# Expert rows written into their experts' regions block by block, with their result's row beside them, instead of an index built after the last block

## The chip, the cores and the metric

The kernel runs on one core of one Trainium2 chip. A core has TensorE (PE), whose weight loads are listed apart as PEld, VectorE (DVE), ScalarE (ACT), GpSimd (POOL) and SyncE (SP). Each runs its own instructions in order and waits for the others by semaphores. The metric is device time in microseconds; the figure before is the median of nine runs. The page beside it is of one profiled execution, and its span reaches from the first to the last instruction.

## What is computed

Float32 throughout: `x` has 4 sequences of 1024 tokens with 128 features, 4096 tokens in all. A modulated layer norm feeds a layer whose small network is trained by gradient steps along the sequence (a scan of 1024 steps, the same for all four sequences), then a second modulated layer norm feeds a mixture of experts: 8 experts with 512 hidden features, the best 2 of each token, and one shared expert for all.

```
h = layernorm(x) * (1 + ca) + sa
k, v = split(h @ W_KV)                       # per token
params = scan(gradient step on mean((mlp(params, k_t) - v_t)**2))
x = x + ga * mlp(params, h @ W_Q)            # mlp = silu(h W1 + b1) W2 + b2

h = layernorm(x) * (1 + cb) + sb
probs = softmax(h @ w_router.T)              # 8 experts
vals, idx = top_k(probs, 2)
gates = one_hot(idx) * vals summed           # 0 for experts not chosen
acc = gelu(h @ Ws1.T + bs1) @ Ws2.T + bs2    # the shared expert
y_e = gelu(h @ W1[e].T + b1[e]) @ W2[e].T + b2[e]
acc = acc + sum over e of gates[e] * y_e
x = x + gb * SCALE * acc
```

## The kernel before

P is 128. The 4096 tokens are 32 columns of 128 tokens, or 8 blocks (`NBLK`) of 512 tokens. The stages, which follow one another:

1. *Front.* Loads, first layer norm, keys and values. Constants are made on POOL in numbered steps (L180 on).
2. *Scan.* 162 iterations of up to 7 steps each, a chain through PE, ACT and DVE. SP issues the loads of Gram products (`gm`, L334) that later iterations need, and groups of keys; the order is written out by hand.
3. *First layer's output, second norm, logits.* A pipeline over the blocks: `mlp_a` (L846) and `mlp_b` (L852) apply the trained network, `residual` (L861) turns the result and adds it to `x_sb`, `ln_stats` (L230) makes mean and `rstd`, with the statistics from DVE and the rest, a power among it, on POOL, `ln_scaled` (L252) and `ln_turned` (L262) make `hT`. `rows` (L870) multiplies each column of `hT` by the identity beside the router weights: one matmul turns the tokens back into rows and gives their logits. The rows go to `h_tab` in DRAM in token order, the logits to `pl`.
4. *Routing.* When all logits are there: softmax, the best two experts by two maxima (`hit`, L955 to L963), running counts of tokens by expert over all columns (`cum`), the place of each (token, choice) pair in an order sorted by expert in which every expert starts a new tile of 128 rows. There are at most `NTL` = 71 tiles. The order is turned round, from place to token, by 128 matmuls `inv` (L1062) of one-hot matrices that DVE builds (`sel` L1048, `val` L1053). `rows_i` is for each place the row of the result table, twice the token plus the choice, and `toks_i` is half of it. Between them PE does the 32 `shared_up` steps (L922), the shared expert's first layer.
5. *Expert loop.* 71 tiles; for tile t: gather its 128 rows from `h_tab` by `toks_i` (L1081, POOL, four tiles ahead), load the expert's two weight matrices (L1090 and L1092, SP, three ahead, the expert read into a register from `whose_i`), turn the rows (`pt` L1099, `xT` L1101), first layer (`ph` L1108, `hs` L1112), second layer (`py` L1120, `yg` L1124), scatter the results to `y_tab` by `rows_i` (L1125, POOL). Four `shared_down` steps (L934; matmuls `ps` L938 and L940, additions L945 and L946), the shared expert's second layer, stand before the loop, and 28 in it, one in every second tile.
6. *Tail.* `y_tab` is loaded back, each token's two results are weighed with its gates and added, and the output is stored.

Stages 3 to 6 stand in `manual_schedule()`: instructions go to the engines in the order of the code. Pools give memory out again when they are closed; an instruction that writes reused memory waits for the former readers. The PSUM pools have three (`pa`), two (`epy`), two (`ept`) and one (`epl`) buffers.

In the loop, before:

```
for t in range(NTL):
    if t + AHEAD < NTL:
        gather(t + AHEAD)
    if t + 3 < NTL:
        ws[t + 3] = weights(t + 3)
    nxt = turn_in(t + 1) if t + 1 < NTL else None
    hs = up(t, xT, ws[t][0])
    if t % 2 and downs:
        shared_down(downs.pop(0))
    if prev:
        down(*prev)
```

Of the kernel before, what the change touches and what calls it, by code (L numbers as in the profile page):

```python
# [10 lines left out]
F32 = mybir.dt.float32  # L11
# [6 lines left out]
P = 128  # L18
# [7 lines left out]
def kernel(  # L26
# [35 lines left out]

    NTL = TOP_K * NTOK // P + NE - 1
    WIN = 32
# [98 lines left out]
    cum = [const.tile([P, NT // 2 + NT, NE], F32, name=f"cum{i}") for i in range(2)]  # L163
# [16 lines left out]
    def constants(n):  # L180
# [27 lines left out]
        elif n == 4:  # L208
            sort_c["lane"] = iota("lane", [P], [[1, P]])
            sort_c["part"] = iota("part", [1], [[0, 1]], mult=1)  # L210
            sort_c["row1"] = iota(
                "row1", [TOP_K, NT], [[1, TOP_K], [TOP_K * P, NT]], base=1, mult=TOP_K
            )
            sort_c["edge"] = iota("edge", [NT], [[P, NT]])
            nc.gpsimd.memset(tri, 1.0)
            nc.gpsimd.affine_select(
                out=tri, in_=tri, compare_op=ALU.is_gt, fill=0.0, base=0, pattern=[[1, P]],
                channel_multiplier=-1,
            )
            for i in range(2):  # L220
                nc.gpsimd.memset(cum[i][:, 0:NT // 2, :], 0.0)
                nc.gpsimd.memset(ends[i][:, 0:NE // 2], 0.0)

# [47 lines left out]
    hT = hpool.tile([P, NBLK, BT], F32, name="hT")  # L271

    with tc.tile_pool(name="scanbig", bufs=1) as sbig, tc.tile_pool(
# [66 lines left out]
        for i, eng in enumerate((nc.gpsimd, nc.vector)):  # L340
            eng.memset(k_rows[i], 0.0)

# [140 lines left out]
        lane, part, row1, edge = (sort_c[n] for n in ("lane", "part", "row1", "edge"))  # L483
# [9 lines left out]
        with tc.tile_pool(name="s_ps", bufs=1, space=PSUM) as sps, tc.manual_schedule():  # L493
# [71 lines left out]
            for i in range(NI):  # L565
# [34 lines left out]
                if i + PF < NI and i:  # L600
                    gms[i + PF] = load_products(i + PF, nc.sync)
                more = todo.pop(0) if todo else None
# [106 lines left out]


# [92 lines left out]
    ffd = ctx.enter_context(tc.tile_pool(name="ffd", bufs=1, space=DRAM))  # L803

    h_tab = ffd.tile([NTOK, D], F32, name="h_tab")
    y_tab = ffd.tile([TOP_K * NTOK, D], F32, name="y_tab")
    with ExitStack() as stage, tc.tile_pool(
# [10 lines left out]


        xg_bufs = [small(f"xg{i}", [D]) for i in range(6)]  # L820
        hit = [small(f"hit{k}", [NT, NE]) for k in range(TOP_K)]
# [4 lines left out]
        gpad = small("gpad", [NT, P // BLK])  # L826
        b2g = small("b2g", [B])
# [3 lines left out]
        nc.gpsimd.memset(gpad, 0.0)  # L831
        nc.gpsimd.memset(gpad[:, :, NE:NX], 1.0)
        for xg in xg_bufs:
            nc.gpsimd.memset(xg, 0.0)


# [5 lines left out]
        ep = stage.enter_context(tc.tile_pool(name="q_sb", bufs=2))  # L842
        pl = small("pl", [NT, NE])
        aq, yq, xh = {}, {}, {}

        def mlp_a(j):  # L846
            pz = bank(pa, "pz", "a", [BT])
            nc.tensor.matmul(pz, lhsT=wqa, rhs=hT[:, j, :], start=True, stop=True)  # L848
            aq[j] = ep.tile([P, BT], F32, name="aq")
# [11 lines left out]
        def residual(j):  # L861
            pyt = bank(ept, "pyt", "t", [BLK, D])
            y = yq.pop(j)
            for i in range(BLK):
                nc.tensor.transpose(pyt[:, i, :], y[:, ts(i, P)], ident)  # L865
            xs = x_sb[:, ts(j, BLK), :]
            nc.vector.tensor_tensor(xs, pyt, xs, ALU.add)
            ln_stats(ep, j)

        def rows(j):  # L870

            hr = ep.tile([P, BLK, D], F32, name="hr")
            for i in range(0, BLK, 2):
# [6 lines left out]
                nc.scalar.copy(hr[:, i:i + 2, :], ptr[:, :, 0:P])  # L880
                c = j * BLK + i
                nc.scalar.copy(pl[:, c:c + 2, :], ptr[:, :, P:P + NE])
            nc.sync.dma_start(
                h_tab[j * BT:(j + 1) * BT, :].rearrange("(c p) d -> p c d", p=P), hr
            )

        for s in range(NBLK + 5):
            if 0 <= s - 2 < NBLK:
                residual(s - 2)
            if 0 <= s - 3 < NBLK:  # L890
                xh[s - 3] = ln_scaled(ep, s - 3)
            if 0 <= s - 4 < NBLK:
                j = s - 4
                ln_turned(bank(ept, "pt", "t", [BT]), xh.pop(j), j, 3, 4, hT[:, j, :])
            if s < NBLK:
                mlp_a(s)
            if 0 <= s - 1 < NBLK:
                mlp_b(s - 1)
            if 0 <= s - 5:
                rows(s - 5)  # L900

        stage.close()
        ep = stage.enter_context(tc.tile_pool(name="e_sb", bufs=2))


        def wide(v_):
            return v_.unsqueeze(2).to_broadcast([P, NT, NE])

        def full(name):
            return small(name, [NT, NE])  # L910

        mx, sm, pr, left, taken = (
            small("mx", [NT]), small("sm", [NT]), full("prob"), full("left"), full("taken")
        )
        nc.vector.tensor_reduce(mx, pl, AX.X, ALU.max)
        nc.vector.tensor_tensor(pr, pl, wide(mx), ALU.subtract)
        nc.scalar.activation(pr, pr, AF.Exp)

# [14 lines left out]

        def shared_down(c):  # L934
# [13 lines left out]
        shared_up(10)  # L948
        nc.vector.tensor_reduce(sm, pr, AX.X, ALU.add)
        nc.vector.reciprocal(sm, sm)  # L950
        nc.vector.tensor_tensor(pr, pr, wide(sm), ALU.mult)
        rest = pr
        for k in range(TOP_K):
            top = gate[:, k, :]
            nc.vector.tensor_reduce(top, rest, AX.X, ALU.max)  # L955
            nc.vector.tensor_tensor(hit[k], rest, wide(top), ALU.is_equal)
            nc.vector.tensor_tensor(hit[k], hit[k], desc.to_broadcast([P, NT, NE]), ALU.mult)
            nc.vector.tensor_reduce(mx, hit[k], AX.X, ALU.max)
            nc.vector.tensor_tensor(hit[k], hit[k], wide(mx), ALU.is_equal)
            if k + 1 < TOP_K:  # L960

                rest = left
                nc.vector.scalar_tensor_tensor(left, hit[k], -4.0, pr, ALU.mult, ALU.add)  # L963

        nc.vector.tensor_tensor(taken, hit[0], hit[1], ALU.add)

        def from_(t, d):
            return t[:, NT // 2 - d:NT // 2 - d + NT, :]

        nc.vector.tensor_copy(from_(cum[0], 0), taken)  # L970
        at, d = 0, 1
        while d < NT:
            nc.vector.tensor_tensor(
                from_(cum[1 - at], 0), from_(cum[at], 0), from_(cum[at], d), ALU.add
            )
            at, d = 1 - at, 2 * d
        inc = from_(cum[at], 0)
        pp = bank(epl, "pp", "l", [2, NE])
        for i, m in enumerate((tri, ones)):
            nc.tensor.matmul(pp[:, i, :], lhsT=m, rhs=inc[:, NT - 1, :], start=True, stop=True)  # L980
        shared_up(10)
        excl = from_(cum[1 - at], 0)
        nc.vector.tensor_tensor(excl, inc, taken, ALU.subtract)
        cnt = small("cnt", [2, NE])
        nc.vector.tensor_copy(cnt, pp)

        over = small("over", [NE, NT])
        nc.vector.tensor_tensor(
            over, cnt[:, 1, :].unsqueeze(2).to_broadcast([P, NE, NT]),
            edge.unsqueeze(1).to_broadcast([P, NE, NT]), ALU.is_gt,  # L990
        )
        tiles = small("tiles", [NE])
        nc.vector.tensor_reduce(tiles, over, AX.X, ALU.add)
        h0 = NE // 2
# [257 lines left out]
```

## Time and profile before

| what | value |
|---|---|
| median of nine runs (lowest to highest) | 924.31 us (923.91 to 932.17) |
| the profiled execution's own time | 924.51 us |
| its span | 922.3 us |
| mean granted TensorE clock | 0.965 |
| PE, DVE, ACT, POOL busy | 88%, 53%, 53%, 63% |
| scan (stage 2) | 60 to 568.6 us of the span |
| stage 3 | 568.6 to 609.3 |
| routing | 609.3 to 654.8 (the first gather) |
| expert loop, first to last `ph` | 664.9 to 884.3 |
| mean of one gather (L1081), one scatter (L1125) | 1025 ns, 1018 ns |

In a view of windows a row is one stretch of time, and for each engine the busy time and number of instructions in it. In a timeline a row is one instruction, or several of one line run together: start, duration, engine, line, what it writes and reads, and in brackets how long the engine had been idle and what ended that. Rows marked SPq or POOLq are an engine's issuing of DMAs. PE's matmuls overlap, so that the start of one to the start of the next tells what one costs.

### The profile page before, as it was taken

The numbers are of one execution on the slowest core, as the hardware profiler recorded it, in microseconds if no ns is written. First come the engines' busy times: TensorE is split into PE (matmuls) and PEld (weight loads), VectorE is DVE, ScalarE is ACT, GpSimd is POOL, SyncE is SP. The second block draws the span as 40 slices with busy tenths as digits, with TensorE's granted clock in tenths as the row PEclk, the third lists the DMA queues.
The fourth block names the chain that finished last, engine by engine and source line by source line (L and its number), as shares of the span: only waits on it lengthen the run. The fifth ranks groups of instructions, "written<-read, shape, count | busy, mean of one in ns | idle before, by whom it ended". The sixth has DMA issues, their size and how long they took to land. (4 is left out here: it accounts for less than half of the span.)

```text
span 922.3 us, 21051 instructions
## 1 busy us (share of the span) xinstructions
PE 808.5 (88%) x6132; PEld 736.4 (80%) x6132; DVE 487.6 (53%) x1843; ACT 491.9 (53%) x1595; POOL 582.6 (63%) x1593
## 2 busy tenths in 40 slices
PE   4689999999999999999999997889888888887740
PEld 3456899999999999999999994546787878887740
DVE  5434566666666666666666663679422221212127
ACT  2554566666666666666666663675233333332333
POOL 6831587778777877787778784520266666666630
PEclk9989999999999999999999998999999999989775
DMA  5363200110001001100011000022056656656655
GB/s 137 104 172 116 82 24 23 24 43 25 23 24 42 25 22 24 42 25 22 24 24 25 21 7 1 27 67 92 29 188 209 202 196 214 216 177 205 197 172 171
DMA packets 77859, 79.84 MB, mean 87 GB/s; under 512 B 9904, under 2 KB 56990, under 8 KB 77744
## 3 DMA queue, kind: packets, MB, share of 16 engines
q1 hardware_dynamic: 68880, 65.58, 23.5%
q0 software_dynamic: 5600, 10.02, 3.7%
q10 hardware_dynamic: 3264, 2.89, 1.0%
q8 instruction: 50, 0.82, 0.4%
q14 instruction: 65, 0.53, 0.2%
HBM read 61.83 MB, written 17.53 MB: 86 GB/s over the span
## 5 line engine op out<-in xcount | busy, mean ns | idle before, releaser
L1112 ACT ACTIVATE hs<-ph,b1t 128x128 f32<-128x128 f32 x284 | 80.8, 370 | 147.8 <-PE pt L1099 80.9
L692 POOL COPY dl<-dz 24x128 f32<-24x128 f32 (+2 forms) x158 | 44.5, 281 | 124.0 <-DVE dz L669 124.0
L1081 POOL DMA_INDIRECT xg<-h_tab,toks_i x71 | 72.8, 1025 | 70.5 <-DVE toks_i L1077 49.1
L1125 POOL DMA_INDIRECT y_tab<-yg,rows_i x71 | 72.3, 1018 | 68.3 <-DVE xT L1101 54.5
L530 DVE SCALAR_TENSOR_TENSOR u<-pu,u 128x130 f32<-128x130 f32 x158 | 46.5, 294 | 112.8 <-PE pu L517 112.8
L1120 PE MATMUL py<-w2t,hs 128*128 128x128 f32 x568 | 80.3, 286 | 18.0 <-issue 12.3
L1108 PE MATMUL ph<-xT,w1t 128*128 128x128 f32 x568 | 80.0, 286 | 13.3 <-DVE xT L1101 13.2
L1120 PEld LDWEIGHTS py<-w2t,hs 128*128 128x128 f32 x568 | 72.0, 198 | 21.8 <-issue 15.4
L1108 PEld LDWEIGHTS ph<-xT,w1t 128*128 128x128 f32 x568 | 71.5, 197 | 19.0 <-DVE xT L1101 19.0
L555 POOL TENSOR_TENSOR sums<-sums,sq 128x48 f32<-128x48 f32 (+2 forms) x315 | 86.3, 293 | 0.0
L633 ACT COPY ad<-z 128x128 f32<-128x128 f32 (+3 forms) x162 | 43.0, 265 | 66.4 <-PE z L631 66.4
L596 PE MATMUL y<-nm,er 128*128 128x128 f32 (+3 forms) x322 | 73.4, 309 | 3.4 <-DVE nm L584 2.7
L498 PE MATMUL z<-kT,a 128*128 128x156 f32 (+3 forms) x324 | 72.9, 307 | 0.0
L539 ACT COPY c<-pv 128x128 f32<-128x128 f32 x158 | 42.0, 266 | 52.7 <-PE pv L535 49.8
L627 PE MATMUL y<-ae,c 128*128 128x128 f32 (+3 forms) x324 | 69.1, 295 | 0.0
L945 DVE TENSOR_TENSOR sh<-ps,gb_rep 128x128 f32<-128x128 f32 x32 | 9.3, 292 | 112.1 <-PE ph L1108 64.5
L508 ACT ACTIVATE vb<-vT,v 128x128 f32<-128x128 f32 (+3 forms) x162 | 65.0, 401 | 1.2 <-DVE dr L656 0.9
L548 POOL TENSOR_TENSOR sq<-ch 128x104 f32<-128x104 f32 (+1 forms) x158 | 56.9, 360 | 12.4
L612 ACT ACTIVATE ae<-z,u 128x156 f32<-128x156 f32 (+3 forms) x162 | 62.8, 388 | 1.9 <-POOL el L693 0.9
L579 PE MATMUL z<-gm,dz 128*128 128x128 f32 (+3 forms) x322 | 62.9, 277 | 0.2
L662 PE MATMUL da<-v,ae 128*128 128x128 f32 (+3 forms) x324 | 62.9, 276 | 0.0
L547 POOL TENSOR_TENSOR ch<-ae 128x104 f32<-128x104 f32 (+1 forms) x158 | 62.4, 395 | 0.0
(294 smaller groups left out, 2433.4 us busy)
## 6 DMA issues: line engine op xcount, KB each, us to landing
w1t<-in_e_w1t_dram SPq DMA_DIRECT2D x71, 256.0 KB
w2t<-in_e_w2t_dram SPq DMA_DIRECT2D x71, 256.0 KB
gm<-g_dram SPq DMA_DIRECT2D x151, 64.0 KB
g_dram<-gw SPq DMA_DIRECT2D x29, 206.0 KB
x_sb<-in_x_dram SPq DMA_DIRECT2D x8, 256.0 KB
k_dram<-kr SPq DMA_DIRECT2D x8, 256.0 KB
h_tab<-hr SPq DMA_DIRECT2D x8, 256.0 KB
hs_all<-y_tab ACTq DMA_DIRECT2D x4, 512.0 KB
```

The costliest lines, as they stand in the source:

```text
L498: nc.tensor.matmul(z[:, 0:n], lhsT=wa, rhs=kc[:, o * B:o * B + n], start=True, stop=alone)
L508: nc.scalar.activation(vb[:, 0:n], vc[:, o * B:o * B + n], AF.Identity, bias=v[:, D:D + 1], scale=-1.0,)
L555: nc.gpsimd.tensor_tensor(t, t, x_[:, :, c0:c1], ALU.add)
L579: nc.tensor.matmul(z[:, 0:rn], lhsT=dz_p[0:ro, :], rhs=gms.pop(i)[0:ro, 0:rn], start=False, stop=True,)
L596: nc.tensor.matmul(y[:, 0:rn], lhsT=er_p[0:ro, :], rhs=nm[0:ro, 0:rn], start=True, stop=False,)
L627: nc.tensor.matmul(y[:, 0:rn], lhsT=wc, rhs=at[:, 0:rn], start=not prev, stop=True)
L662: nc.tensor.matmul(da[0:rn, :], lhsT=et[:, 0:rn], rhs=v[:, 0:D], start=not prev, stop=True)
L1081: nc.gpsimd.indirect_dma_start(out=xg_bufs[t % 6][:], out_offset=None, in_=h_tab[:, :], in_offset=bass.IndirectOffsetOnAxis(ap=toks_i[:, t ...
L1108: nc.tensor.matmul(ph[:, f, :], lhsT=w1t[:, ts(f, P)], rhs=xT, start=True, stop=True)
L1112: nc.scalar.activation(hs[:, f, :], ph[:, f, :], AF.Gelu_apprx_tanh, bias=b1t[:, t, f:f + 1])
L1120: nc.tensor.matmul(py, lhsT=hs[:, f, :], rhs=w2t[:, f, :], start=(f == 0), stop=(f == NFC - 1))
L1125: w = nc.gpsimd.indirect_dma_start(out=y_tab[:, :], out_offset=bass.IndirectOffsetOnAxis(ap=rows_i[:, t:t + 1], axis=0), in_=yg[:], in_off ...
```

## The change

*Regions.* `h_tab` is replaced by `h_sort`, a DRAM table with a region of 4096 rows for each expert and 128 rows more. A row has 144 values: the 128 features and 16 times the number of the row of the result table (`HW = D + 16`). A `blank` tile, whose rows hold zeros and a row number outside the result table, is written over all of `h_sort` in 33 transfers (`fill`); 16 more (`together`) copy each expert's first and second layer side by side into `e_all` in DRAM. These 49 transfers are issued by SP in the scan, one in every third iteration from the ninth on.

*Routing by blocks.* Stages 3 and 4 become one loop over the blocks. After the logits of a block, `choose` finds the best two experts from the logits themselves, `rank` gets each pair's place from the counts of this block and those carried from the blocks before (matmuls with `tri` and `ones`), `send` scatters the rows of the block from SBUF to their places, eight indirect DMAs of 128 rows by POOL, and `count` carries the counts on. The statistics of the second norm are all on DVE (`stats`, the inverse root by a bit trick and three Newton steps), its scaling on ACT (`turned_rows`). `rows` copies each row twice, once for each choice, into one of five buffers `hrs`, whose last 16 columns hold the result's row. All 32 `shared_up` steps stand in this loop. Softmax, gates and the tables of tiles come after it; the place-to-token matmuls and their one-hot matrices are gone.

*The loop.* A tile's rows are 128 rows of `h_sort` in order: SP loads them from a place read into a register, as it loads both layers' weights with one DMA from `e_all`. `to`, the row numbers for the result's scatter, is copied from the rows themselves. Weights and rows are fetched four tiles ahead. 16 `shared_down` steps stand before the loop and 16 in it, spread evenly.

```diff
@@ constants
+            nc.gpsimd.memset(blank, 0.0)
+            nc.gpsimd.memset(blank[:, :, D:HW], float(4 * TOP_K * NTOK))
@@ before the scan
+        def fill(n):
+            r0, r1 = n * P * FILL, min((n + 1) * P * FILL, NE * NTOK + P)
+            nr = (r1 - r0) // P
+            nc.sync.dma_start(
+                h_sort[r0:r1, :].rearrange("(p r) d -> p r d", r=nr), blank[:, 0:nr, :]
+            )
+        def together(n):
+            e, k = n // 2, n % 2
+            nc.sync.dma_start(
+                e_all[:, e, k * NFC * P:(k + 1) * NFC * P],
+                e_w2t[:, e, :, :].rearrange("p c d -> p (c d)") if k else e_w1t[:, e, :],
+            )
@@ in the scan
+                if early_work and i >= 9 and i % 3 == 0:
+                    do, n = early_work.pop(0)
+                    do(n)
@@ the pool of stages 3 and 4
+        qp = ExitStack()
+        ep = qp.enter_context(tc.tile_pool(name="q_sb", bufs=2))
+        HR = 5
+        hrs = [ep.tile([P, BLK, TOP_K, HW], F32, name=f"hr{i}", bufs=1) for i in range(HR)]
@@ stats, in place of ln_stats
+            for i in range(BLK):
+                nc.vector.bn_stats(st[:, i, :], x_sb[:, j * BLK + i, :])
+            for i in range(BLK):
+                nc.vector.bn_aggr(ag[:, i, :], st[:, i, :])
...
+            for _ in range(3):
+                nc.vector.tensor_tensor(t, r[at], r[at], ALU.mult)
+                nc.vector.scalar_tensor_tensor(t, t, -0.5, var, ALU.mult, ALU.mult)
+                nc.vector.scalar_tensor_tensor(r[1 - at], t, 1.5, r[at], ALU.add, ALU.mult)
+                at = 1 - at
@@ rows
-                nc.scalar.copy(hr[:, i:i + 2, :], ptr[:, :, 0:P])
-            nc.sync.dma_start(
-                h_tab[j * BT:(j + 1) * BT, :].rearrange("(c p) d -> p c d", p=P), hr
-            )
+                nc.scalar.copy(
+                    hrs[j % HR][:, i:i + 2, :, 0:D],
+                    ptrs[i // 2][:, :, 0:P].unsqueeze(2).to_broadcast([P, 2, TOP_K, D]),
+                )
@@ choose, for each of the two choices
+                nc.vector.tensor_reduce(top, rest, AX.X, ALU.max)
+                nc.vector.tensor_tensor(hit, rest, over_e(top), ALU.is_equal)
+                nc.vector.tensor_tensor(hit, hit, desc.to_broadcast([P, BLK, NE]), ALU.mult)
+                nc.vector.tensor_reduce(first, hit, AX.X, ALU.max)
+                nc.vector.tensor_tensor(hit, hit, over_e(first), ALU.is_equal)
@@ rank
+            nc.tensor.matmul(rk, lhsT=tri, rhs=taken[j], start=True, stop=False)
+            for d in range(1, BLK):
+                nc.tensor.matmul(
+                    rk[:, d:BLK, :], lhsT=ones, rhs=taken[j][:, 0:BLK - d, :],
+                    start=False, stop=False,
+                )
+            nc.tensor.matmul(rk, lhsT=ones, rhs=carry[j], start=False, stop=True)
@@ send
+            for i in range(BLK):
+                for k in range(TOP_K):
+                    w = nc.gpsimd.indirect_dma_start(
+                        out=h_sort[:, :], out_offset=bass.IndirectOffsetOnAxis(
+                            ap=place_i[:, k, i:i + 1], axis=0
+                        ),
+                        in_=hrs[j % HR][:, i, k, :], in_offset=None,
+                        bounds_check=NE * NTOK - 1, oob_is_err=False,
+                    )
@@ the order of stages 3 and 4
+        for j in range(NBLK):
+            choose(j)
+            rank(j)
+            if j + 1 < NBLK:
+                turned_rows(j + 1)
+            if j + 3 < NBLK:
+                mlp_b(j + 3)
+            if j >= 1:
+                shared_up(2)
+            if j + 1 < NBLK:
+                rows(j + 1)
+            if j + 2 < NBLK:
+                added(j + 2)
+            send(j)
+            count(j)
+            if j + 2 < NBLK:
+                stats(j + 2)
+            if j + 3 < NBLK:
+                residual(j + 3)
+            if j >= 1:
+                shared_up(3)
@@ after softmax, gates and the tables of tiles
+        qp.close()
+        ep = stage.enter_context(tc.tile_pool(name="e_sb", bufs=2))
@@ the loop's loads
-            nc.gpsimd.indirect_dma_start(
-                out=xg_bufs[t % 6][:], out_offset=None, in_=h_tab[:, :],
-                in_offset=bass.IndirectOffsetOnAxis(ap=toks_i[:, t:t + 1], axis=0),
-                bounds_check=NTOK - 1, oob_is_err=False,
-            )
+        def weights(e):
+            wt = ep.tile([P, 2, NFC, P], F32, name="wt", bufs=5)
+            nc.sync.dma_start(
+                wt.rearrange("p k f d -> p (k f d)"),
+                e_all[:, bass.ds(e, 1), :].rearrange("p e f -> p (e f)"),
+            )
+            return wt
+        def tokens(at):
+            xg = ep.tile([P, HW], F32, name="xg", bufs=6)
+            nc.sync.dma_start(xg, h_sort[bass.ds(at, P), :])
+            return xg
@@ turn_in
+            to = ep.tile([P, 1], I32, name="to", bufs=6)
+            nc.vector.tensor_copy(to, xg[:, D:D + 1])
@@ the loop
+        LATE = 16
+        vals = [values(t) for t in range(AHEAD)]
+        ws = {t: weights(vals[t][0]) for t in range(AHEAD)}
+        xs = {t: tokens(vals[t][1]) for t in range(AHEAD)}
+        for c in range(NT - LATE):
+            shared_down(c)
+        downs = list(range(NT - LATE, NT))
+        cur = turn_in(xs.pop(0))
+        for t in range(NTL):
+            if t + AHEAD < NTL:
+                e, at = values(t + AHEAD)
+                ws[t + AHEAD] = weights(e)
+                xs[t + AHEAD] = tokens(at)
+            nxt = turn_in(xs.pop(t + 1)) if t + 1 < NTL else None
+            hs = up(t, cur[0], ws[t])
+            if downs and (t + 1) * LATE // NTL > LATE - len(downs):
+                shared_down(downs.pop(0))
+            if prev:
+                down(*prev)
```

## The prediction

> **What bounds the kernel now.** I read the page's slices first (TensorE, PE below, is busy nine tenths of almost every slice), then the busy time by stage, then the timeline inside the stages that the change touches. The windows below begin at the end of the scan; columns are engine busy time with instruction counts, granted clock, DMA share and GB/s.
>
> ```profile
> core 0: us, PE busy (x) PEld busy (x) DVE busy (x) ACT busy (x) POOL busy (x), PEclk, DMA share, GB/s
> 568.60:609.30 40.70, 34.90 (x163) 21.86 (x164) 21.17 (x73) 23.38 (x55) 20.39 (x64) 0.92 0.14 40
> 609.30:655.00 45.70, 42.00 (x195) 26.14 (x195) 39.34 (x77) 23.86 (x36) 0.18 (x1) 1.00 0.18 58
> 655.00:665.00 10.00, 7.74 (x56) 6.26 (x55) 3.06 (x11) 2.34 (x4) 6.04 (x6) 1.00 0.14 39
> 720.00:760.00 40.00, 33.16 (x269) 30.49 (x267) 9.10 (x38) 13.75 (x49) 24.79 (x25) 1.00 0.62 200
> ```
>
> The first two rows are what the change fuses: 86.4 us in which PE is busy 76.9 and POOL nearly idles in the second half. The fourth is the expert loop: the clock is full, DMA works 62% of the time, and PE still shows seven microseconds of idling in forty. Its matmul records overlap in their modelled ends, so the true slack is read from starts:
>
> ```profile
> 722.52 0.30 PEld L938 LDWEIGHTS ps<-eb,gT 128*128 128x128 f32 x2
> 722.85 1.06 PE L940 MATMUL ps<-sw,hs_all 128*128 128x128 f32 x8
> ...
> 723.63 0.97 PEld L1120 LDWEIGHTS py<-w2t,hs 128*128 128x128 f32 x8
> ...
> 724.52 0.14 PEld L1099 LDWEIGHTS pt<-iw,xg 128*128 128x128 f32 x1
> 724.63 0.27 PE L1099 MATMUL pt<-iw,xg 128*128 128x128 f32 x1
> 724.64 0.97 PEld L1108 LDWEIGHTS ph<-xT,w1t 128*128 128x128 f32 x8
> ...
> 725.64 1.02 POOL L1081 DMA_INDIRECT xg<-h_tab,toks_i  x1 [0.31 <-issue]
> 725.98 0.29 DVE L945 TENSOR_TENSOR sh<-ps,gb_rep 128x128 f32<-128x128 f32 x1 [4.01 <-PE ph L1108]
> ...
> 727.72 1.14 ACT L1112 ACTIVATE hs<-ph,b1t 128x128 f32<-128x128 f32 x4 [3.69 <-PE pt L1099]
> ```
>
> From start to start a shared down costs PE 723.63 − 722.52 = 1.11 us, four `py` pairs 724.52 − 723.63 = 0.89, a `pt` 0.12, four `ph` pairs 0.89 again: a tile is 1.90. The first `ph` starts at 664.9 and the last at 884.3: 219.4 us for 70 steps and 28 downs, of which PE needs 70 × 1.90 + 28 × 1.11 = 164.1. So 55.3 us, 0.79 a step, is waiting. The last lines show on what: `ps` is over at 723.9 but DVE reads it at 725.98, `ph` of 724.74 is over by 725.8 but ACT starts at 727.72. PE's completions reach the other engines about 2 us late. In the stage before the loop, with as busy a PE, `ph` of the shared expert ends at 652.02 and ACT starts at 652.05. What differs is POOL's indirect DMAs, two a tile in the loop, back to back:
>
> ```profile
> 658.95 1.00 POOL L1081 DMA_INDIRECT xg<-h_tab,toks_i  x1 [0.30 <-issue]
> 660.26 1.00 POOL L1081 DMA_INDIRECT xg<-h_tab,toks_i  x1 [0.30 <-issue]
> 661.56 1.00 POOL L1081 DMA_INDIRECT xg<-h_tab,toks_i  x1 [0.30 <-issue]
> ```
>
> During this row of gathers, with no other traffic to speak of, a `ps` already waited 1.8 us for DVE (ended 661.7, read 663.49). That the indirect DMAs cause the lateness is inference; that it goes with them is what the trace shows.
>
> **The change, part by part.** *Front and scan.* 49 more transfers go through SP's queue in the scan, one every third iteration: 33 of 590 KB that blank `h_sort` and 16 of 256 KB, DRAM to DRAM, that put both layers of an expert side by side. The scan is a chain PE, ACT, DVE of 2.96 us an iteration, with DMA mostly idle (slices 6 to 23: tenths of 0 to 2). Iterations that load 337 KB of keys took 2.897 or 2.985 us beside 2.897 without: 0 to 0.09 each. For 49 transfers that is 0 to 4.4 us; on SP one issue of 0.3 to 0.45 us precedes loads that are fetched iterations ahead. Two memsets of 128x1152 on POOL in the front are, by the 0.95 us of a 128x1024 one, 0 to 2 us. I take 2.2 for all of it, both ends kept.
>
> *The fused stage.* Per block of 512 tokens DVE gets choose (12 operations of about 0.21 at 128x32), the residual add 0.69, statistics (8 of 0.28 and less, 13 of 0.21, in place of POOL's chain with its 1.04 us power), send and count (5 of 0.21): 8.5 us. ACT gets 8.2 (four scaled rows 1.2, `hT` 0.78, four copies 1.6, `aq` and `yq` 1.5, four shared activations of 0.69, blank ids), PE 8.4. The 128 `inv` matmuls (15.4 us of PE), the 21.7 us of `sel` and `val` on DVE, and the stores of `h_tab` go. POOL gets eight scatters a block, each 128 rows of 576 B. A gather or scatter of 128 rows has a period of 1.30 to 1.33 us here, so 64 cost 64 × 1.32 = 84.5 us: 10.6 a block, more than any other engine. POOL bounds this stage. Block 0's logits are out at 590.35 before; in the new order I add aq, yq, pyt, add, stats, rows from the same rows and reach 586, then choose 2.5, rank 1.2, send 0.6: first scatter at about 591.5, last one over at 591.5 + 84.5 = 676, landed at 678. PE, ACT and DVE are done by about 655; the tile bookkeeping (11 us of small DVE operations, two table loads of 1.28) hides under the scatters.
>
> *Between the stages.* The working buffers close after the bookkeeping, and the loop's pool reuses the memory of the five row buffers. In the built order the loop's first weight load on SP, the first `sh` and the first `hs` each wait for all eight of POOL's DMA semaphores, that is for the 64th scatter. So of the 16 shared downs before the loop PE can place two (the PSUM buffers) and the rest follow 678: 14 to 16 × 1.11 = 15.5 to 17.8 us. Under these lie the four weight loads and four token loads, about 8 to 10 us. First `ph` at 694 to 696, so 695 against 664.9: **30.1 us later**.
>
> *The loop.* Downs fall from 28 to 16, PE needs 70 × 1.90 + 16 × 1.11 = 150.8. POOL's gathers go: one indirect DMA a tile instead of two. SP has two register loads (0.52 to 0.76 each, load to next issue) and two issues of 0.33 a tile, 1.8 to 2.2, up to 2.5 with the semaphore work. DMA moves the same weights and 72 KB of rows instead of 64; by 0.62 × 3.2 us it needs 2.0 us a tile. With the waiting halved like the indirect DMAs (0.39 a step) the 70 steps take 178.1, 2.54 each; by SP alone 2.2 to 2.5. I take 2.50: 175.0, **44.4 us less**. The bounds are 2.2 (154) and the old waiting kept whole, 150.8 + 55.3 = 206.1.
>
> *Weights in one run* cost nothing by themselves: packets of 2048 B took 99 ns and the 4096 B ones of POOL's queue 200, the same per byte, so I give longer runs no gain; if they had one, DMA is covered by the 2.5 anyway.
>
> The Trainium skill ("DMA: Bandwidth & Descriptors", section "Rules for kernel authors") says to coalesce small transfers into large ones, with best bandwidth from 1 MiB per DMA. By it the one load of 512 KB would gain; by the packets above it gains nothing, and I follow the packets.
>
> The Trainium skill ("SBUF — State Buffer", section "SBUF: two separate sides") speaks against this change: a DMA issued from GpSimd needs its descriptors written, and one that takes 620 ns alone took some 3100 beside a VectorE copy holding the shared port. The 64 scatters now lie beside VectorE's busiest stretch. By its figure as an estimate they would take 64 × 3.1 = 198 us; the loop here shows periods of 1.33 with VectorE copies beside them, against 1.30 without, so I stay with 1.32.
>
> *The tail* (combine, output stores, from 884 on: 38 us) is the same code.
>
> *Sum*, against the profiled execution's own 924.51 (span 922.3 and 2.2 around it; the median of nine runs is 924.31): + 2.2 + 30.1 − 44.4 = −12.1, so **912**. Break-even is a loop of 219.4 − 32.3 = 187.1 us, 2.67 a step.
>
> **The rivals.**
>
> *A, slower: the late completions stay.* If lateness goes with DMA load rather than with the count of indirect ones (the loop's share rises from 0.62 to about 0.8 when it runs at 2.5), each step keeps 0.79 of waiting: 206.1 us, last `ph` at 901 instead of 884, 924.5 + 2.2 + 30.1 − 13.3 = **943**. It decides from 2.67 us a step. For it: the longest gaps of the loop (around 850 and 866) lie where no shared down remains to fill them, and 12 fewer remain. Against it: the lag already exists at 661 with gathers alone and no other traffic.
>
> *B: late completions pace the fused stage.* It has PE to ACT to PE to DVE to PE chains in each block, and indirect DMAs run beside all of it. A delay of 2 us on each of PE's completions, as in the loop, carried through the same order of operations puts the landing at 700 instead of 678: 912 + 22 = **934**. At 1 us it is 682, so it needs nearly the loop's full lag; the loop has other traffic beside it, this stage little.
>
> *C: the loop comes near its floor.* With one indirect DMA a tile POOL has pauses, completions are prompt, and 2.2 us a step remain: 924.5 + 32.3 − 65.4 = **891**. For it: no lateness in the scan and the front under ordinary queues. Against it: SP's and DMA's 2.0 to 2.5.
>
> *D: the scan gives way.* If the blanking transfers, 18.9 MB, delay the `gm` loads or lengthen the chain by twice what the key loads do, 49 × 0.18 = 8.8: 912 + 6.6 = **919**, no visible change. The reloads are fetched ahead, which speaks against it.
>
> **How the numbers follow.** What a measurement can tell from no change is about 0.5%, 4.6 us. I give the forecast 0.42, A 0.20, B 0.14, C 0.17, D 0.07. The forecast's own range, loop of 2.4 to 2.6 a step, is 903 to 921. Faster takes most of the forecast (0.36), C, and a little of D: 0.55. Slower takes A, B and the tail of the forecast: 0.37. The rest, 0.08, is no change. For 8 in 10 the range reaches to the lower side as far as 887 and to the upper as far as 944, A whole.
>
> **What would show it.** Scan: an iteration period still near 2.96 with the extra transfers. Fused stage: POOL's scatters at 1.32 from about 591 to 676 without gaps; gaps between blocks mean B. Between: the first loop weight load issued only after the last scatter lands, and the first `ph` near 695; if it comes much before, the reuse of memory isn't what holds it and I am too pessimistic. Loop: the period between `ph` groups near 2.5 and DVE reading `ps` sooner after its end than 2 us; still 2 us late means A. The forecast is wrong altogether if the loop's steps exceed 2.67 or the first `ph` comes after 710.

## The result and the profile after

The changed kernel takes 939.55 us (median of ten runs, 935.38 to 945.71) against 924.31 (median of 31 runs, 920.78 to 932.17). By the means of these runs, as in all ratios below, it takes 1.0149 times the time before, with a 95% interval of 1.0121 to 1.0176: it is slower, by 1.5%. The forecast was 912, and 939.55 lies between the two rivals on the slower side (934 and 943).

The profiled execution is longer than all ten, 949.04 us with a span of 947.0 (24.7 more than before). The first view is by stretches: fused stage, between its last scatter and the loop, and the loop.

```profile
core 0: us, PE busy (x) PEld busy (x) DVE busy (x) ACT busy (x) POOL busy (x), PEclk, DMA share, GB/s
605.00:706.00 101.00, 68.40 (x254) 39.39 (x252) 52.50 (x274) 52.44 (x104) 62.55 (x64) 0.83 0.14 47
706.00:730.40 24.40, 21.07 (x164) 20.56 (x164) 10.92 (x39) 2.07 (x3) 0.00 (x0) 0.85 0.35 127
740.00:780.00 40.00, 34.39 (x293) 32.74 (x292) 11.40 (x53) 17.17 (x61) 15.10 (x16) 1.00 0.86 256
```

The 64 scatters are spread over 101 us in which no engine is full, not even POOL. In the loop DMA has gone from 0.62 to 0.86 busy and POOL from 24.8 to 15.1 us in forty. A step of the loop, from the timeline, shows that the late completions are gone there:

```profile
748.66 0.33 PE L1228 MATMUL pt<-iw,xg 128*128 128x128 f32 x1 [0.93 <-DMA xg<-h_sort]
...
749.95 1.06 PE L1199 MATMUL ps<-sw,hs_all 128*128 128x128 f32 x8
...
751.04 0.29 DVE L1204 TENSOR_TENSOR sh<-ps,gb_rep 128x128 f32<-128x128 f32 x1 [1.67 <-PE ps L1199]
```

`ps` ends at 751.01 and DVE reads it at 751.04. Over the whole loop this wait has a median of 0.04 us; before it was 2.08. What PE waits for now is in the first line, the tile's rows. The timeline of the fused stage shows where the lateness went:

```profile
617.68 0.22 DVE L942 TENSOR_TENSOR tq<-r 128x4 f32<-128x4 f32 x1 [0.87 <-DVE r L944]
...
619.10 0.16 DVE L943 SCALAR_TENSOR_TENSOR tq<-tq,varq 128x4 f32<-128x4 f32 x1 [1.21 <-DVE tq L942]
...
620.50 0.16 DVE L944 SCALAR_TENSOR_TENSOR r<-tq,r 128x4 f32<-128x4 f32 x1 [1.24 <-DVE tq L943]
...
679.09 0.39 PE L1015 MATMUL rk<-carry,ones 128*128 128x32 f32 x2
...
683.80 0.22 DVE L1030 TENSOR_TENSOR at<-hits,rk 128x64 f32<-128x64 f32 x1 [5.67 <-PE ph L1059]
```

The rank of a block is done at 679.48 and DVE uses it at 683.80, 4.3 us late. The trace also holds the semaphores' updates, the signals by which an engine tells that an instruction is done: six of PE's instructions end between 679.4 and 683.2, and their six updates stand together at 683.77 to 683.95. (That is why the bracket names a later instruction of PE, `ph`.) So the signals came late, and not the reader. Even DVE's chain on its own results, operations that elsewhere follow each other at 0.20 us, runs for a while at 1.4, close to the period of one scatter (1.28). Late places make POOL idle between blocks:

```profile
624.10 0.97 POOL L1040 DMA_INDIRECT h_sort<-hr,place_i  x1 [0.30 <-issue]
634.46 0.97 POOL L1040 DMA_INDIRECT h_sort<-hr,place_i  x1 [9.39 <-DVE st L928]
```

The logits of the third block are read 5.4 us late, and this pause of POOL follows. The ranks of the next four blocks are read 3.7, 4.1, 2.8 and 4.3 us late, and POOL pauses 3.14, 3.15, 1.71 and 3.25 us. These five pauses, less the usual 0.30 each, are 19.1 us. The granted clock is 0.83 in the first window and falls to 0.50 in parts of it, but these four ranks and the ends of these logits stand where it was 1.00.

From the timelines (us of the span; the scan's end is the start of its last activation; the forecast's times are without its 2.2 us for the scan, its span is with them):

| kernel | scan's end | first scatter | last scatter over | first `ph` | last `ph` | span |
|---|---|---|---|---|---|---|
| before | 559.2 | | | 664.9 | 884.3 | 922.3 |
| changed | 570.7 | 604.7 | 705.9 | 730.4 | 907.5 | 947.0 |
| changed, forecast | 559.2 | 591.5 | 676 | 695 | 870 | 910 |

The first `ph` is 65.5 us later, the loop 42.3 shorter (177.1 against 219.4), the tail 1.5 longer: 65.5 − 42.3 + 1.5 = 24.7, the difference of the spans.

### The profile page after: what moved, and what is told of

Same layout as the page of the kernel before. It is cut to its first block, busy times and chain, and to the rows that moved or that the text cites. A ratio compares the mean times of both kernels' runs of the same rounds, so it can differ in the third digit from the quotient of the medians.

```text
span 947.0 us, 21438 instructions
## 1 busy us (share of the span) xinstructions
PE 821.5 (87%) x6082; PEld 738.4 (78%) x6082; DVE 504.0 (53%) x2110; ACT 510.9 (54%) x1633; POOL 552.1 (58%) x1531
## 5 line engine op out<-in xcount | busy, mean ns | idle before, releaser
L1256 POOL DMA_INDIRECT y_tab<-yg,to x71 | 69.0, 972 | 138.5 <-DVE to L1232 89.5
L728 POOL COPY dl<-dz 24x128 f32<-24x128 f32 (+2 forms) x158 | 44.4, 281 | 133.2 <-DVE dz L705 133.2
L1040 POOL DMA_INDIRECT h_sort<-hr,place_i x64 | 62.8, 982 | 60.3 <-DVE st L928 37.6
L1239 PE MATMUL ph<-xT,wt 128*128 128x128 f32 x568 | 75.4, 276 | 0.7 <-DVE to L1232 0.7
L1251 PE MATMUL py<-wt,hs 128*128 128x128 f32 x568 | 74.9, 275 | 0.0
L1239 PEld LDWEIGHTS ph<-xT,wt 128*128 128x128 f32 x568 | 68.8, 191 | 0.9 <-DVE to L1232 0.9
L1251 PEld LDWEIGHTS py<-wt,hs 128*128 128x128 f32 x568 | 69.0, 192 | 0.0
L1255 DVE COPY yg<-py 128x128 f32<-128x128 f32 x71 | 20.7, 292 | 80.2 <-PE py L1251 80.2
L682 PE MATMUL da<-ad,hm 128*128 128x128 f32 (+3 forms) x322 | 63.2, 278 | 0.0
```

The source lines that it names most:

```text
L682: nc.tensor.matmul(da[0:rn, :], lhsT=hm[0:ro, 0:rn], rhs=ad_p[0:ro, 0:D], start=True, stop=False,)
L1239: nc.tensor.matmul(ph[:, f, :], lhsT=wt[:, 0, f, :], rhs=xT, start=True, stop=True)
L1251: nc.tensor.matmul(py, lhsT=hs[:, f, :], rhs=wt[:, 1, f, :], start=(f == 0), stop=(f == NFC - 1))
L1256: w = nc.gpsimd.indirect_dma_start(out=y_tab[:, :], out_offset=bass.IndirectOffsetOnAxis(ap=to, axis=0), in_=yg[:], in_offset=None, bounds ...
```

## The experiments

They ran on four chips, and the kernel before was run on each again: it took 884.5, 882.6 and 885.5 us on the first three and 924.8 on the fourth. So there are chips on which the kernel before takes 884, and some on which it takes 924, as in the run that the prediction was made from. Each chip was used on one occasion only, so what belongs to the chip and what to the occasion isn't separated; "kind of chip" stands for both. Whether the fourth was the very chip of that first run isn't known. Ratios below are to the kernel before on the same chip; where single profiles of two chips are compared, both are of the kind that takes 884, unless the text says otherwise.

**The changed kernel again** (no edit).

> The changed kernel as it is, for a second profile. In the first one the granted clock fell to 0.5 between 80 and 90 us, before any of the added transfers, and the scan started its steady part 11.5 us later than before, 3.6 of them already at its first iteration. If that dip is an accident of the execution, this profile shows iteration 10 about 3.6 us later than before and not 11.5, and a time of 935 to 946. If the change brings the dip (through the work it adds to the front), it shows 11.5 again.

Measured: 914.94 us where before takes 884.5 (one execution; 3.4% slower). Scan's end 557.9, first scatter 593.0, last over 675.1, first `ph` 696.4, last `ph` 873.6, span 912.9. The clock stayed at 1.00 between 80 and 90 us and the scan's first iterations took their usual time. The windows are those of the fused stage and the loop:

```profile
593.00:676.00 83.00, 65.24 (x276) 40.13 (x274) 54.66 (x280) 55.10 (x107) 62.92 (x64) 0.90 0.18 58
720.00:760.00 40.00, 34.89 (x292) 32.77 (x291) 11.12 (x51) 17.55 (x62) 15.20 (x16) 1.00 0.85 253
```

The same 64 scatters take 82.1 us here, not 101.2; the loop is the same, 177.2. A rank, and DVE's use of it, here:

```profile
619.17 0.39 PE L1015 MATMUL rk<-carry,ones 128*128 128x32 f32 x2
...
619.59 0.22 DVE L1030 TENSOR_TENSOR at<-hits,rk 128x64 f32<-128x64 f32 x1 [0.79 <-PE rk L1015]
```

All eight ranks are read 0.04 us after their end. The time expected, 935 to 946, missed because this chip is of the other kind, and iteration 10 came 1.2 us earlier than before, not 3.6 later. The dip of the clock to 0.50 near 80 us comes in some executions and not in others. It also came in both runs of the kernel before with other results (below), which hold none of the 49 transfers. And the first figures of the prediction (591.5, 676, 695) are this kernel's, on a chip where completions are prompt.

**Scatters written behind the last block in the code.**

```diff
+            places[j] = place_i
+
+        def issue(j):
+
+            place_i = places.pop(j)
             for i in range(BLK):
                 for k in range(TOP_K):
...
+        for j in range(NBLK):
+            issue(j)
```

> All 64 scatters stand behind the last block's other work instead of behind each block (eight row buffers instead of five). Theory: while POOL issues indirect DMAs, completions of the other engines arrive late, and this stretches a block of the fused stage from 8.5 us to 13. Then the blocks now follow each other at 8.5 to 9.5 us, the last place_i comes about 65 us after the first (88 in the changed kernel), the scatters follow without gaps at 1.28, 82 us, and the execution takes 35 to 45 us longer than the changed kernel. Rival: the order written out by hand makes a chain of 13 us a block whatever POOL does. Then the last place_i is still some 88 us after the first and the execution takes 65 to 75 us longer.

Measured: 917.98 us, the first scatter at 593.3 and the last over at 675.6. Both expectations missed, because the edit holds nothing back: POOL has nothing else in its queue at this point, and each scatter waits for its own places only. It shows merely that eight row buffers do no better than five.

**30 shared downs in the loop.**

```diff
-        LATE = 16
+        LATE = 30
```

> 30 shared downs in the loop instead of 16, 2 before it. Theory: the loop of the changed kernel is held by its transfers (DMA busy 85 to 89 percent, 2.53 us a step), PE has slack there. Then the loop stays within 3 us of 177 although PE gets 15.5 us more work in it, it starts 8 us earlier (as soon as the first weights and rows land), and the kernel is 6 to 10 us faster than the changed one, about 931. Rival: PE's chain paces the loop; then it grows by 10 to 15 us and the kernel is 2 to 7 us slower than the changed one.

Measured: 914.25 us (912.78 to 921.17), 1.0345 times before (1.0284 to 1.0405), so no better than the unedited kernel. First `ph` 686.9, 12.5 us earlier after the scan's end than in the repeat; but the loop took 186.2. Each theory had half of it: the start came earlier, and of 15.5 us more work for PE in the loop, 9 came out as time.

**One part alone: weights in one run, in the kernel before.**

```diff
-            nc.sync.dma_start(w1t, e_w1t[:, bass.ds(e, 1), :].rearrange("p e f -> p (e f)"))
-            w2t = ep.tile([P, NFC, D], F32, name="w2t", bufs=4)
+            wt = ep.tile([P, 2, NFC, P], F32, name="wt", bufs=4)
             nc.sync.dma_start(
-                w2t, e_w2t[:, bass.ds(e, 1), :, :].rearrange("p e c d -> p (e c) d")
+                wt.rearrange("p k f d -> p (k f d)"),
+                e_all[:, bass.ds(e, 1), :].rearrange("p e f -> p (e f)"),
```

> The kernel before with only one part of the change: both layers' weights put side by side in the scan by 16 transfers, and loaded with one DMA a tile. Theory: packets cost the same per byte and the loop waits for late completions, so the time stays within 0.4 percent of 924.3 and the loop's first to last ph at 216 to 222 us. Rival: half the issues and packets on SP's queue relieve the loop; then its steps shorten by 0.1 us or more, 7 us in all, 917 or less.

Measured: 1.0025 times before (0.9992 to 1.0059), loop 182.5 us. The figures expected stood on 924, the chip gave 884; against the loop of before on such a chip, 182.4 in the next run, the edit changes nothing. Packets of 4096 B took 216 ns in this loop, those of 2048 B 103 in the next run's, so they cost no less per byte. But POOL paces this loop, as the next runs show, and so a gain of SP's or of DMA's would hardly show in its time.

**The kernel before again** (no edit).

> The kernel before, for its profile beside the next three. The first four runs had it at 884.5 us, the nine shown first at 924.3; in the profiles at hand the whole difference of such a kind lies where POOL issues indirect DMAs (loop 219.4 against 182.5 with both layers in one run). If this one takes about 884, its loop is 180 to 185 us and DVE reads ps within 0.3 us of its end; if about 924, the loop is near 219 and ps is read up to 2 us late.

Measured: 884.43 us, loop from 662.2 to 844.7, 182.4 us. It is faster than in the first profile almost wholly in the loop, by 37.0 of the 40.2 us between the spans. The windows of 720 to 760 us of this run, and POOL's timeline in it:

```profile
720.00:760.00 40.00, 36.96 (x320) 35.89 (x321) 11.88 (x44) 16.11 (x57) 30.83 (x31) 1.00 0.78 243
```

```profile
720.61 1.02 POOL L1125 DMA_INDIRECT y_tab<-yg,rows_i  x1 [0.30 <-issue]
721.93 1.02 POOL L1081 DMA_INDIRECT xg<-h_tab,toks_i  x1 [0.31 <-issue]
723.26 1.02 POOL L1125 DMA_INDIRECT y_tab<-yg,rows_i  x1 [0.31 <-DVE x_sb L946]
```

POOL never rests: two indirect DMAs a tile at 1.33 or a little less are 2.6 us, and 70 steps of 2.6 are 182. With prompt completions POOL sets the pace of the old loop. `ps` is read 0.04 us after its end.

**The changed kernel without any indirect DMA.** It leaves out the 64 scatters, so that all regions stay blank, and stores each tile's results in tile order.

> The changed kernel without the 64 scatters (every region stays blank) and with each tile's result stored by SP in tile order instead of scattered. Theory: POOL's scatters bound the stage where completions are prompt, and delay completions where they are not. Without them the last place_i comes 62 to 66 us after the first, and the first ph comes 16 to 22 us after that one's end of the bookkeeping, at 675 to 685 with a scan as in the last runs (696 with scatters, 730 in the first profile). Rival: the bookkeeping and the 16 shared downs, not the scatters, set the loop's start; then the first ph stays within 5 us of 696.

Measured: first `ph` at 691.1 with the scan's end at 562.0, which is 129.1 us after it; with scatters (repeat) it is 138.5. So the scatters delay the loop by 9.4 us only: the last places come 64 us after the first, the bookkeeping takes until 670, and then come the 16 shared downs. Theory and rival both hold a part. The loop took 201.6. PE's waits for the rows rose to 47.2 us (26.4 in the repeat): SP, which issues them, now also waits for each tile's result before its store, 14 us between 700 and 880. Whether that is the whole of the 24 us more wasn't tested.

**Scatters held back in fact**, by places copied once after the last block, again with eight row buffers; run on both kinds of chip.

```diff
-                            ap=place_i[:, k, i:i + 1], axis=0
+                            ap=spots[1][:, j, k, i:i + 1], axis=0
...
+        nc.vector.tensor_copy(spots[1], spots[0])
+        for j in range(NBLK):
+            issue(j)
```

> All 64 scatters take their places from one tile that DVE copies after the last block, so that none runs beside the blocks. The blocks then run without indirect DMAs: 9.0 to 9.3 us each on every execution. Theory of the bound: the scatters take 82 us back to back and the first ph moves from 696 by what they start later, some 63 us, to 755 to 765; time 975 to 985 where before takes 884. In a state with late completions the same blocks would have taken 13 us; if they take 9 in it, POOL's indirect DMAs are what stretched them.

Measured where before takes 883: 977.74 us, scatters from 656.5 to 738.1, first `ph` 759.1, all as expected. The whole delay of the scatters, 61.2 us against the scan's end, came through (60.4 in the first `ph`).

> Scatters held until the last block, once more, in case this call lands where before takes about 924. There the changed kernel's blocks took 13 us; if POOL's indirect DMAs are what stretches them, they take 9.0 to 9.5 us here, the row of 64 scatters then runs beside the bookkeeping alone, and the loop takes 177 to 182. If the blocks stay at 12 or more, the lateness on that chip has another cause. Where before takes 884 it repeats 977.7 within 1 percent.

Measured where before takes 924.8: 978.54 us. The windows of the blocks, and of the scatters:

```profile
593.00:658.00 65.00, 59.92 (x257) 34.98 (x256) 45.75 (x258) 51.42 (x102) 0.00 (x0) 0.97 0.00 1
658.00:740.00 82.00, 7.59 (x31) 6.58 (x30) 8.99 (x31) 5.15 (x8) 62.52 (x64) 0.54 0.17 57
```

The eight blocks are done in 65 us with PE nearly full, on a chip of the kind on which they took some 13 us each with scatters beside them: from the first places to the last it is 62.4 us here, 88.2 in the first profile of the changed kernel and 63.1 in the repeat. All eight ranks are read 0.04 us after their end. The held kernel costs the same on both kinds, 977.7 and 978.5, while before costs 883 and 925. So what stretches the blocks is the running of POOL's indirect DMAs beside them. (The changed kernel itself wasn't run on the fourth chip.)

**The kernel before with results stored in tile order by SP**, one indirect DMA a tile instead of two; also on both kinds of chip. The rows of the result table are then not where the tail looks for them, so this kernel serves to measure the loop only: it leaves out the placing of the results, and its output isn't the layer's.

```diff
-            w = nc.gpsimd.indirect_dma_start(
-                out=y_tab[:, :], out_offset=bass.IndirectOffsetOnAxis(
-                    ap=rows_i[:, t:t + 1], axis=0
-                ),
-                in_=yg[:], in_offset=None, bounds_check=TOP_K * NTOK - 1, oob_is_err=False,
-            )
+            nc.sync.dma_start(to[ts(n, P), :], yg)
```

> The kernel before, its tiles' results stored by SP in tile order instead of scattered by POOL: one indirect DMA a tile instead of two. Where before takes 924, the theory of late completions gives a loop of 185 to 200 instead of 219, a time near 900. Where before takes 884, PE already paces the loop (steps of 1.90 and 3.01) and the loop stays at 178 to 188 us.

Measured where before takes 883: 877.03 us, loop 167.5. The expectation missed: it took the loop for PE's, and it was POOL's, worth 15 us. The whole time fell by 5.6 us only: both this execution and the next have the dip of the clock near 80 us, 8.0 and 6.5 us ahead of the loop.

> Before with results stored in tile order by SP, once more. Where before takes 924: with half of the indirect DMAs gone the loop falls from 219 to 170 to 200 and ps is read less late. Where before takes 884 the loop stays at 165 to 170 as in the first such run, against 182.4 with two indirect DMAs a tile, which is 70 times 2 times their period of 1.30.

Measured where before takes 924.8: 876.38 us, loop 168.1. Without half of the indirect DMAs the loop of that kind of chip is 51 us shorter (219.4 in the first profile), and all difference between the chips is gone. The window of its loop, and POOL in it:

```profile
700.00:740.00 40.00, 40.00 (x361) 40.00 (x360) 12.46 (x48) 18.89 (x67) 16.40 (x17) 1.00 0.88 269
```

```profile
719.06 1.00 POOL L1082 DMA_INDIRECT xg<-h_tab,toks_i  x1 [2.02 <-PE pt L1100]
720.95 1.00 POOL L1082 DMA_INDIRECT xg<-h_tab,toks_i  x1 [0.90 <-PE pt L1100]
```

PE is full, and POOL rests 1 to 2 us between its DMAs. `ps` is read 0.04 us after its end (median of 28, 0.40 at most).

**Rows fetched earlier in the changed loop.** In the repeat, PE's waits for the rows are the loop's longest on PE (columns: engine and line, what it waited for, us, times, longest):

```profile
PEld pt L1228 <- DMA xg<-h_sort: 26.4, 39, 1.3
...
PE pt L1228 <- DMA xg<-h_sort: 18.4, 29, 1.2
```

```diff
+        AHEAD_X = 9
...
+            if t + AHEAD_X < NTL:
+                xs[t + AHEAD_X] = tokens(value(t + AHEAD_X, 1))
+            if t + AHEAD < NTL:
+                ws[t + AHEAD] = weights(value(t + AHEAD, 0))
```

> The changed kernel, each tile's rows fetched nine tiles ahead instead of four and issued before the weights (eleven buffers); the loop's order is otherwise the same. Theory: where completions are prompt, the changed loop is held by the rows, which queue behind 512 KB of weights (26 us of its 177 are PE waiting for xg). Then the loop takes 153 to 163 us instead of 177 and the kernel gains 14 to 24 us on the changed one, 891 to 901 where that takes 915. Rival: DMA itself is the bound (busy 84 to 90 percent in the loop); then the loop stays above 170.

Measured: 902.70 us (899.69 to 905.43), 1.0179 times before (1.0114 to 1.0244); loop 162.8. The theory holds for the loop; the time is 1.7 us above what was expected. The loop's DMA rises to 0.91 busy:

```profile
710.00:750.00 40.00, 38.20 (x334) 37.16 (x334) 11.76 (x59) 20.06 (x71) 16.50 (x18) 1.00 0.91 277
```

> As the run before, with the rows of the first tile issued ahead of all weights and 30 shared downs in the loop instead of 16. PE needs 166 us in the loop then. Theory: the loop starts at 681 to 686 instead of 696 and takes 168 to 176; its last ph is at 852 to 860 (873 in the changed kernel), the time 893 to 901. Rival: if DMA paces the loop it ends no earlier than in the run before, some 868, about 908. Either way it does not beat the 884 of before on a chip where before takes that.

Measured with first rows ahead of all weights and `LATE = 30`: 903.74 us (897.26 to 908.33), 1.0184 times before (1.0092 to 1.0277); the loop starts 123.4 us after the scan's end (136.8 in the run before) and takes 174.0. Its first `ph` at 693.4 and last at 867.4 lie 7 us past the expected ranges, in an execution that has the dip (8 us); the median lies 2.7 past. The start came 13.4 us earlier and the loop took 11.2 longer: the downs cost in the loop nearly what they cost ahead of it. No version found beats the kernel before where that takes 884; where it takes 924 these two were not run.

## Why the prediction was wrong

- *The sum.* The profiled span is 36.8 us longer than the forecast one (947.0 against 910.2): 9.3 in the scan, 1.7 from there to the first scatter, 16.7 in the row of scatters, 5.5 from its end to the first `ph`, 2.1 in the loop, 1.5 in the tail. The median of ten runs lies 9.5 below this execution.
- *What bounds the old loop.* Right for the profile at hand: late completions, going with POOL's indirect DMAs. The prediction called that an inference; the held scatters and the tile-order results show it, on a chip that has the lateness. Of the 55.3 us of waiting, though, only 37.0 (219.4 − 182.4) go with the lateness; the rest stays with prompt completions, where POOL's two DMAs a tile pace the loop.
- *Scan.* 2.2 us forecast. From its eleventh iteration to its last the scan takes 449.4 us in both first profiles; the 49 transfers cost nothing. The 11.5 us of the profile after are 3.6 ahead of the first iteration (later runs of the changed kernel began at 66.5 to 70.6, before at 67.7 and 67.5) and 8.0 in the first ten iterations, where the clock dips. Half of the ten runs (935.4 to 937.9) lie some 6 us below the other half (941.2 to 945.7), at a higher mean clock (0.947 to 0.953 against 0.941 to 0.946); whether the dip makes this difference no trace shows. The prediction's row of 337 KB, 2.897 and 2.985 us isn't in the trace: iterations take 2.96, and beside a load of some 400 KB of keys 2.96 to 3.05, so that its bound of 0.09 a transfer stands.
- *Fused stage.* **This is the step that failed:** "64 cost 64 × 1.32 = 84.5 us ... POOL bounds this stage". In the execution it was 101.2 us, and POOL paused five times for places that came late. Against the repeat with prompt completions the first `ph` came 34.0 us later, of which 12.8 stand in the scan, 19.1 in the row of scatters (101.2 − 82.1), 3.2 behind it, less 1.1 ahead of it. It is rival B, which had 0.14. It was set aside with "it needs nearly the loop's full lag; the loop has other traffic beside it, this stage little". That was the wrong quantity: the stage has little traffic, but 64 indirect DMAs nearly end to end, beside chains that take 9.1 us a block when prompt, and its lag was no less than the loop's 2 us: 2.8 to 4.3 on four ranks. B's own price, a landing 22 us later, is close: against the scan's end the last scatter was over 18.4 us later than forecast. (The forecast's first scatter is itself mis-added: 586 + 2.5 + 1.2 + 0.6 is 590.3, not 591.5.)
- *Between the stages.* 16 downs after the last scatter: the first `ph` 24.5 us after it against 19 forecast, 21.3 in the repeat. That the scatters hold the loop's start was right one for one when they were held back, but without any the start comes only 9.4 us earlier; the bookkeeping stands close behind.
- *Loop.* −44.4 forecast, −42.3 measured; 2.53 us a step against 2.50. The size was right in part by luck. Waiting did not just halve: completions became prompt, and the rows behind 512 KB of weights in SP's queue took their place, worth 14.4 us (177.2 to 162.8) where before takes 884.
- *Weights in one run at nothing:* the time agrees, 1.0025 (0.9992 to 1.0059), in a loop that POOL paces. The Trainium skill's rule for merging transfers ("DMA: Bandwidth & Descriptors", section "Rules for kernel authors") brought nothing there, and the packets of twice the size took twice the time (216 ns against 103).
- *The warning of the Trainium skill* ("SBUF — State Buffer", section "SBUF: two separate sides") that a DMA of GpSimd may take five times as long beside a VectorE copy: the scatters kept 1.28 us beside VectorE's operations of this stage on both kinds of chip. What suffered were the other engines' completions.
- *The other kind of chip.* The forecast was made for chips like that of the result. Where completions are prompt the old loop takes 182.4 and not 219.4. There the loop gains 5.2 us, the start comes 34 later, and the change was 3.4% slower (one execution), although first scatter, last scatter, first `ph` and loop each came within 3 us of the forecast.

## What to carry to other kernels

When a change takes a disturbing kind of instruction out of one stage and puts it into another, price the same disturbance where it goes, beside what runs there, before counting the gain. Count the slow instruction over the whole kernel: before, 142 indirect DMAs; after, 135, of which 64 now stand ahead of the loop where little else can start. And what is fetched late in one queue is fetched behind everything issued before it: small loads that the next step needs first go out early.

## What the runs showed of the hardware

On some chips completions came late while POOL issued indirect DMAs end to end, and on others they did not, with the same kernel, the same 1.28 to 1.33 us a DMA and, from 720 to 760 us, a clock of 1.00: before takes 924 or 884, and its `ps` is read 2.08 us late (median) or 0.04. It reaches DVE's own chain too. It does not appear with one indirect DMA in 2.4 us (168.1 and 167.5 on the two kinds), and the first five to ten of a row show little of it.

What makes the difference between the chips isn't settled. One more mark of it stands in the traces. In the four from chips where before takes 924, some of the semaphores' updates of PE, ACT and DVE aren't recorded (about 210 in before, 340 in the changed kernel, 190 and 175 in the held and the tile-order kernel), all of them between the first and the last indirect DMA; in the ten other traces hardly one is missing. Every run whose span is on record carries the profiler's clock too, and none is known to have run without recording. So a rival stays open: that the recording has a part in the lateness there.

The granted clock falls to 0.50 for 17 to 21 us, from 71 to 75 us on, in four of the 14 profiles, of either kernel, and the first ten iterations of the scan then take 6.5 to 8 us longer. PE is busy meanwhile, so it isn't a pause of PE that makes the dip last. The window of 80 to 90 us of the first run with tile-order results, a kernel that has nothing of the change in it:

```profile
80.00:90.00 10.00, 10.00 (x35) 6.58 (x34) 2.44 (x11) 2.71 (x11) 0.00 (x0) 0.50 0.24 71
```
